# The partner rows of a rotary rotation: VectorE's shuffle, or two transfers from SBUF to SBUF

## The chip, the cores and the metric

The kernel runs on one core of a Trainium2 chip. A core has a matrix engine (TensorE, PE in the profile, with its weight loads as PEld), a vector engine (VectorE, DVE), an activation engine (ScalarE, ACT), GpSimd (POOL) and SyncE (SP), from whose queue (SPq) all transfers of this kernel are issued. Each engine runs its own list of instructions in order, and semaphores make one wait for another. Data lies in SBUF, 128 partitions wide; TensorE writes its results to banks of PSUM.

The metric is the device time of one execution in microseconds, the median of several runs. All arithmetic is in float32.

## The reference

Two transformer layers on an input of 2 x 1024 tokens with 512 features. In each layer the attention (16 heads of 32 features, causal) and a gated feed-forward block both read the same normalised input, and both results are added to x:

```python
x = L0_attn_X                                   # (2, 1024, 512)
xn = _layernorm(x, axis=-1)
x = x + attn0(xn) + ffn0(xn)                    # hidden width 2048
xn = _layernorm(x, axis=-1)
x = x + attn1(xn) + ffn1(xn)                    # hidden width 1408, scaled ternary weights
```

Queries and keys are rotated by position before the scores. The two layers pair the 32 features of a head in different ways:

```python
# layer 0: neighbours are a pair
x0 = x[..., 0::2]; x1 = x[..., 1::2]
r0 = cos * x0 - sin * x1
r1 = sin * x0 + cos * x1
return jnp.stack((r0, r1), axis=-1).reshape(x.shape)

# layer 1: feature d and feature d + 16 are a pair
x1, x2 = (x[..., :half], x[..., half:])
return jnp.concatenate([x1 * cos - x2 * sin, x1 * sin + x2 * cos], axis=-1)
```

Then follow `softmax(q k^T / sqrt(32))` under the causal mask, the product with the values, and the output projection.

## The kernel before

**Stages.** A phase is one layer for one of the two batch rows: four phases, layer 0 first. In each phase the 16 heads are worked in four groups of four, so that a group's 4 x 32 features fill the 128 partitions. Queries and keys are kept transposed, with features on the partitions and tokens along the columns: `qT` holds 512 tokens of a group in one tile, `kT` all 1024. A group's scores come in blocks of 256 queries, a block in steps of 256 keys: 10 steps for each group, 40 for each phase, 160 in all (class `Run`). A step makes the scores on TensorE (`sc`), copies them to SBUF (`s`), finds row maxima (`rmax`), subtracts them and takes exponentials. Five steps later (`LAG`) the weighted sums `av` are formed on TensorE. The row maxima of a block go out to DRAM (`md`) and come back spread over all partitions (`mb`), two transfers from SyncE's queue.

**Filling in.** Between the steps, the class `Fill` gives TensorE the rest of the phase's work: the projections to queries and keys (class `QueriesKeys`), to values, the hidden units of the feed-forward block (class `Hidden`), the down-projections `d` and the output projections. The projections and hidden units share the form `Unit`: four pieces, `first` to `fourth`, which get the four blocks of a product from seven half-size products of sums and differences. Intermediate results are copied from a PSUM bank by ScalarE into one of four buffers of 128x512 (`keep`, pool `t5_p`, names `p`, `u`, `raw`), while TensorE goes on to accumulate into the same bank.

**The rotation.** A `QueriesKeys` unit yields four tiles of 128x512 for a group: queries and keys, for the first and the second 512 tokens. Each goes through `rotated` (lines 864 to 880). `raw` is the tile of unrotated rows, one of the four `t5` buffers. For each group of 32 partitions, VectorE's `stream_shuffle` (line 877) writes into `swapped` (one of two buffers) the row's partner: the neighbour in layer 0, the row 16 further in layer 1, from the table `SWAP` (line 49). Then GpSimd multiplies `raw` by the cosines in place (line 878), VectorE multiplies `swapped` by the signed sines (line 879), and GpSimd adds both into `qT` or `kT` (line 880). There are four phases, four groups in each and four tiles in each group, thus 64 rotations. The first four (names `raw_k` and `raw_q`) come from `project_qk` at the start of the kernel; the 60 others come from the 15 units, with `raw` called `p_qk` (twice), `u_qk` and `raw_qk`. In the profile `swapped` is `sw_q` or `sw_k`. The tables of cosines and sines come from `rope_tables` (line 1761).

**The order of the work.** No order is written by hand for the engines. The class `Schedule` records each operation with the operations that it depends on, gives it a cost from a formula (`cost`, line 187), and lays out two plans by simulating the five engines: a first one while the program is being recorded, and a second one at its end (`again`, line 358), which orders each engine's queue by due times worked back from TensorE's ideal sequence. The instructions are then emitted in the order of the second plan's start times. Lines 208 and 209 hold the planned cost of a shuffle, 735 ns; line 193 that of a transfer: 450 ns of SyncE, and 1900 ns plus the bytes divided by 345 per ns until it lands, to which line 162 adds 900 ns until another engine sees it. The second plan may move GpSimd's additions to VectorE when they are late (`either`), and may bring forward one of the next seven pieces of TensorE's work when the next one would wait over 300 ns. A `View` (line 52) carries the region of a tile that an operation touches; `apart` (line 151) tells two regions that have nothing in common.

Of the kernel before, what the change touches and what calls it, by code (L numbers as in the profile page):

```python
# [19 lines left out]
B, T, D, H = 2, 1024, 512, 16  # L20
DH = D // H
# [22 lines left out]
def ts(n, size):  # L44
    return slice(n * size, (n + 1) * size)

SWAP = ([d ^ 1 for d in range(DH)], [(d + DH // 2) % DH for d in range(DH)])


class View:
# [5 lines left out]
    def __getitem__(self, idx):  # L58
        idx = idx if isinstance(idx, tuple) else (idx,)
        idx = idx + (slice(None),) * (len(self.shape) - len(idx))  # L60
        shape, region = [], []
        for n, i in zip(self.shape, idx):
            if isinstance(i, slice):
                a, b, _ = i.indices(n)
                shape.append(b - a)
                region.append((a, b))
            else:
                region.append((i, i + 1))
        return View(self.tile, self.chain + [("__getitem__", (idx,), {})], shape, self.region if self.chain else region)

    def rearrange(self, pattern, **sizes):
# [83 lines left out]
class Schedule:  # L155
# [31 lines left out]
    def cost(self, eng, method, args, kwargs, outs, ins):  # L187

        n = self.columns(outs[0]) if outs else 0
        if eng is self.sync:  # L190

            size = 4 * int(np.prod((outs or ins)[0].shape, dtype=int))
            return 450.0, 1900.0 + size / self.RATE
        if eng is self.tensor:
            if method == "transpose":
                mode, t = "full", 131.0
            else:
                lhs, rhs = args[1], args[2]
                small_k, small_m = lhs.shape[0] < P, lhs.shape[1] < P
                mode = "rows" if small_k else "columns" if small_m else "full"  # L200
                t = max(self.columns(rhs), 64) * 1.676 / (1 if mode == "full" else 4)
            if mode != self.mode:
                t += {"full": 218.0, "columns": 100.0, "rows": 200.0}[mode]
                self.mode = mode
            return t, t + 163.0
        m = max([n] + [self.columns(i) for i in ins])
        if eng is self.vector:
            if method == "stream_shuffle":
                t = 735.0
            elif method == "reciprocal":  # L210
                t = 204.0
            elif method == "tensor_reduce" and not kwargs.get("apply_transpose"):
                t = (150.0 if ins[0].tile.pool.psum else 110.0) + m * (0.93 if ins[0].tile.pool.psum else 1.85)
            elif method == "bn_aggr":
                t = 182.0
            else:
                t = 160.0 + m * 1.04
        elif eng is self.scalar:
            t = (190.0 if method == "activation" and args[2] in self.TABLES else 150.0) + 0.85 * n
            for k in ("bias", "scale"):  # L220
                t += 105.0 if isinstance(kwargs.get(k), View) else 0.0
            t += 140.0 if method == "mul" else 0.0
        elif method == "affine_select":
            t = 150.0 + 0.95 * n
        elif method in ("memset", "tensor_copy"):
            t = 100.0 + 1.16 * n
        else:
            t = 184.0 + 2.12 * n
        return t - self.BESIDE[eng.name], t
# [276 lines left out]
def two_layers(ctx: ExitStack, tc: tile.TileContext, x_in, attn_w, ffn_w, ffn_s, rope, out):  # L506
    ctx.enter_context(tc.manual_schedule())
    nc = Schedule(tc.nc)
# [64 lines left out]
    phases = [(layer, b) for layer in range(2) for b in range(B)]  # L573
# [288 lines left out]
    turned = {}  # L862

    def rotated(ph, g, which, half, raw):
        layer, _ = phases[ph]
        turned[ph, g] = turned.get((ph, g), 0) + 1
        name = f"{which}{ph}_{g}_{half}"
        if which == "q":
            dst = qT[ph, g, half] = q_p.tile([P, TB], F32, tag="q", name=f"{name}T")
        else:  # L870
            if (ph, g) not in kT:
                kT[ph, g] = k_p.tile([P, T], F32, tag="k", name=f"k{ph}_{g}T")
            dst = kT[ph, g][:, ts(half, TB)]
        cos, sin = tables[ph]
        cols = ts(half, TB)
        swapped = tmp.tile([P, TB], F32, tag="swapped", name=f"sw_{name}")
        nc.vector.stream_shuffle(swapped, raw, SWAP[layer])
        nc.gpsimd.tensor_tensor(raw, raw, cos[:, cols], ALU.mult)
        nc.vector.tensor_tensor(swapped, swapped, sin[:, cols], ALU.mult)
        nc.gpsimd.tensor_tensor(dst, raw, swapped, ALU.add)  # L880
# [3 lines left out]
    def project_qk(which, tokens):  # L884

        half, at = divmod(tokens.start, TB)
        n = tokens.stop - tokens.start
        ps = bank(f"ps_{which}0_{tokens.start}", (P, n))
        for c in range(DC):
            nc.tensor.matmul(  # L890
                ps, wqk[0, 0, which][:, c, :], xnT[0, half][:, c, at : at + n], start=(c == 0), stop=(c == DC - 1)
            )
        if tokens.stop == T:
            load_next_wqk(0, 0, which)
        if at == 0:
            raws[which] = t5_p.tile([P, TB], F32, tag="t5", name=f"raw_{which}0_{half}")
        nc.scalar.copy(raws[which][:, at : at + n], ps)
        if at + n == TB:
            rotated(0, 0, which, half, raws[which])

    class QueriesKeys(Unit):
# [11 lines left out]
        def c11(self, bank, one):  # L913
            nc.vector.tensor_tensor(one, bank, one, ALU.add)
            rotated(self.ph, self.g, "q", 0, one)

        def c22(self, bank, k1):
            nc.vector.tensor_tensor(k1, bank, k1, ALU.add)
            rotated(self.ph, self.g, "k", 1, k1)
# [496 lines left out]
    class Fill:  # L1416
# [14 lines left out]
        def add(self, cost, fn, kind="other", unit=None, slice_=0):  # L1431
            self.main.append((cost, fn, kind, unit, slice_))
# [40 lines left out]
        def do_main(self, step):  # L1473
            cost, fn, kind, unit, _ = self.main.pop(0)
            if kind == "first":
                self.unit = unit
            fn()
            if kind == "second":
                self.decide(step)
            if cost and kind != "alone":  # L1480
                self.turn = True
            return cost
# [196 lines left out]
    for i in range(total + LAG):  # L1679
        ph = min(i // per_phase, len(phases) - 1)  # L1680
# [5 lines left out]
        run, n = steps[i] if i < total else (None, 0)  # L1686
# [74 lines left out]
def rope_tables():  # L1761

    pos = np.arange(T, dtype=np.float32)
    half = np.arange(DH // 2, dtype=np.float32)
    base = np.float32(10000.0)
    freq0 = np.power(base, np.float32(-2.0) * half / np.float32(DH))
    freq1 = np.float32(1.0) / np.power(base, half / np.float32(DH // 2))
    d = np.arange(P) % DH
    tables = []
    for freq, pair, first in ((freq0, d // 2, d % 2 == 0), (freq1, d % (DH // 2), d < DH // 2)):  # L1770
        angles = (freq[pair][:, None] * pos[None, :]).astype(np.float32)
        sign = np.where(first, -1.0, 1.0).astype(np.float32)[:, None]
        tables.append(np.stack([np.cos(angles), np.sin(angles) * sign]))
    return np.ascontiguousarray(np.stack(tables), dtype=np.float32)

# [37 lines left out]
```

## Time and profile before

Three runs took 1810.8, 1814.7 and 1815.25 us; the median is 1814.7. The profiled execution:

| | us | share of the span |
|---|---|---|
| span of the profiled execution | 1812.9 | |
| TensorE busy (PE) | 1798.0 | 99% |
| VectorE busy (DVE) | 1476.3 | 81% |
| GpSimd busy (POOL) | 1232.6 | 68% |
| ScalarE busy (ACT) | 1041.7 | 57% |
| TensorE's granted clock, mean | 0.998 | |
| share of the 16 DMA engines' time, SyncE's queue | | 28.5% |

The profile page gives the span from the first to the last instruction; it has no figure for the time around it.

How to read it: the lines of groups name an engine, an operation, the tile written and the tiles read, the shape and the count, and then the busy time in us, the mean duration in ns, and the time for which the engine stood idle just before such instructions, with what ended it. All instructions recorded by `Schedule` carry the same line, L278, as its `call` issues them; so one goes by the tiles' names. A matmul of 512 columns in float32 appears as two instructions. The durations of matmuls contain the time in the pipeline, so two in a row overlap.

### The profile page before, as it was taken

Reading aid. Unit: us, or ns where it says so; the run is one execution under the profiler, and the core shown is the slowest. Engines: PE = TensorE matmul, PEld = TensorE weight load, DVE = VectorE, ACT = ScalarE, POOL = GpSimd, SP = SyncE. Lnnn points to the kernel's source line nnn. Section 1 sums busy time; section 2 is a strip of 40 time slices with the busy share of each in tenths; the row PEclk is TensorE's granted clock in tenths of the full one; section 3 lists DMA queues with packets and bytes.
Section 4 is the critical chain, followed back from the end, with each engine's and each line's share of the span. In section 5 each row is a group of like instructions: output and inputs, shape, how many; then the busy total and the mean of one; then the engine's idle time right before and its main releaser. Section 6 shows DMA issues by size and latency. Waiting matters only on the chain.

```text
span 1812.9 us, 25807 instructions
## 1 busy us (share of the span) xinstructions
PE 1798.0 (99%) x9406; PEld 880.0 (49%) x9406; DVE 1476.3 (81%) x1975; ACT 1041.7 (57%) x1240; POOL 1232.6 (68%) x1145
## 2 busy tenths in 40 slices
PE   9999999999999999999999999999999999999998
PEld 5464444444444644444444455444444464444443
DVE  3665988868879668779697798888979998989988
ACT  2444665556546565554575556576565757565762
POOL 6726875956868337446377894886779775866775
PEclk9999999999999999999999999999999999999999
DMA  5324343222232422222133324222223322221211
GB/s 192 99 82 137 114 148 120 67 80 82 80 113 88 138 72 68 70 82 89 56 97 102 115 76 160 76 80 71 77 84 98 125 69 71 70 69 50 67 39 71
DMA packets 140334, 165.15 MB, mean 91 GB/s; under 512 B 13360, under 2 KB 93488, under 8 KB 140208
## 3 DMA queue, kind: packets, MB, share of 16 engines
q1 hardware_dynamic: 140208, 163.50, 28.5%
q8 instruction: 75, 1.23, 0.3%
q14 instruction: 51, 0.42, 0.1%
HBM read 134.62 MB, written 28.84 MB: 90 GB/s over the span
## 4 chain that ended last, share of the span: by engine, by line
PE 89%; POOL 5%; DVE 3%; issue 1%; ACT 1%; DMA 1%; SPq 0%; POOLq 0%; ACTq 0%; DVEq 0%
PE d L278 24%; PE ux L278 19%; PE uy L278 9%; PE sc L278 8%; PE av L278 7%; PE ux_qk L278 5%; PE uz L278 5%; POOL acc L278 2%; PE uy_qk L278 2%; PE ux_v L278 2%; PE uz_qk L278 1%; PE uy_v L278 1%; DVE s L278 1%; PE ps_o L278 1%; PE tr L278 1%
## 5 line engine op out<-in xcount | busy, mean ns | idle before, releaser
L278 POOL TENSOR_TENSOR acc<-acc,s 128x512 f32<-128x512 f32 (+1 forms) x378 | 487.4, 1311 | 84.4 <-ACT s L278 79.9
L278 DVE TENSOR_TENSOR s<-s,mb 128x512 f32<-128x512 f32 (+1 forms) x384 | 489.6, 1300 | 12.5 <-DMA mb<-md 12.5
L278 DVE TRANSPOSE_TENSOR_REDUCE rmax<-s 128x32 f32<-128x1024 f32 (+1 forms) x320 | 351.5, 1117 | 63.9 <-POOL s L278 41.3
L278 PE MATMUL d<-wd,hT 128*128 128x512 f32 x864 | 400.1, 593 | 0.0
L278 ACT ACTIVATE s<-s 128x1024 f32<-128x1024 f32 (+1 forms) x320 | 304.9, 970 | 163.0 <-DVE s L278 161.0
L278 ACT ACTIVATE s<-sc 128x1024 f32<-128x1024 f32 (+1 forms) x320 | 283.3, 934 | 195.1 <-PE sc L278 184.0
L278 POOL TENSOR_TENSOR acc<-s 128x512 f32<-128x512 f32 (+1 forms) x128 | 169.2, 1328 | 195.3 <-ACT s L278 191.5
L278 PEld LDWEIGHTS d<-wd,hT 128*128 128x128 f32 x864 | 161.9, 190 | 192.6 <-issue 186.9
L278 ACT ACT_TABLE_LOAD x167 | 214.3, 1283 | 7.7 <-DVE s L278 4.7
L278 DVE TENSOR_TENSOR x<-d,x 128x512 f32<-128x512 f32 x224 | 151.3, 676 | 75.8 <-PE d L278 75.0
L278 PE MATMUL av<-s,v 128*32 128x256 f32 (+1 forms) x2560 | 159.2, 364 | 0.7 <-ACT s L278 0.5
L278 POOL TENSOR_SCALAR_AFFINE_SELECT s<-s 128x512 f32<-128x512 f32 x128 | 98.9, 784 | 67.0 <-ACT s L278 65.0
L278 PEld LDWEIGHTS av<-s,v 128*32 128x32 f32 x2560 | 67.6, 109 | 145.7 <-issue 97.2
L278 POOL TENSOR_TENSOR hT<-p,hT 128x512 f32<-128x512 f32 x53 | 72.5, 1367 | 77.9 <-ACT hT L278 77.9
L278 PE MATMUL d<-wo,oT 128*128 128x512 f32 x198 | 103.0, 602 | 1.2 <-DVE hT L278 1.2
L278 PE MATMUL ux<-xs,ws 128*128 128x512 f32 x212 | 101.7, 602 | 0.6 <-ACT p L278 0.6
L278 PE MATMUL ux<-xnT,wu 128*128 128x512 f32 x212 | 101.8, 602 | 0.1
L278 PE MATMUL ux<-xnT,wg 128*128 128x512 f32 x212 | 100.9, 598 | 0.4 <-DVE hT L278 0.4
L278 PE MATMUL ux<-xs,wu 128*128 128x512 f32 x212 | 101.2, 600 | 0.0
L278 PE MATMUL uy<-xs,ws 128*128 128x512 f32 x212 | 99.7, 593 | 0.3 <-DVE hT L278 0.3
L278 PE MATMUL uy<-xnT,ws 128*128 128x512 f32 x212 | 99.8, 593 | 0.0
L278 PE MATMUL uz<-xnT,wg 128*128 128x512 f32 x212 | 99.7, 593 | 0.0
(179 smaller groups left out, 2511.2 us busy)
## 6 DMA issues: line engine op xcount, KB each, us to landing
mb<-md SPq DMA_DIRECT2D x64, 512.0 KB, 3.8
wg<-in_gate SPq DMA_DIRECT2D x54, 256.0 KB, 2.9
wd<-in_down SPq DMA_DIRECT2D x32, 256.0 KB, 2.9
xr<-xm SPq DMA_DIRECT2D x32, 256.0 KB, 2.7
wu<-in_up SPq DMA_DIRECT2D x28, 256.0 KB, 3.0
s12gu<-ws SPq DMA_DIRECT2D x26, 256.0 KB, 2.0
ws<-s12gu SPq DMA_DIRECT2D x26, 256.0 KB, 2.6
wd<-wds SPq DMA_DIRECT2D x22, 256.0 KB, 2.9
```

Source lines behind the costliest of these rows:

```text
L278: target(*[get(a) for a in args], **{k: get(a) for k, a in kwargs.items()})
```

## The change

The shuffle is replaced by two transfers on SyncE's queue. The first writes the even rows of `swapped` from the odd rows of `raw`, the second the odd rows from the even ones: 64 rows of 2 KB each. For this the partner of every row has to be its neighbour in both layers. So the columns of the second layer's query and key weights are laid out on the host so that features d and d + 16 of a head become neighbours, and the tables of cosines and sines use the layer 0 arrangement for both; scores are sums over the features of a head, which the order of the features doesn't alter. `View` learns steps, so that the plan sees the two transfers as touching different rows, and the planned cost of the shuffle is dropped. The transfers get the planned cost of any other transfer.

```diff
-SWAP = ([d ^ 1 for d in range(DH)], [(d + DH // 2) % DH for d in range(DH)])
...
     def __getitem__(self, idx):
...
             if isinstance(i, slice):
-                a, b, _ = i.indices(n)
-                shape.append(b - a)
+                a, b, step = i.indices(n)
+                shape.append(len(range(a, b, step)))
                 region.append((a, b))
+                if step > 1:
+                    parity = (a % step, a % step + 1)
...
+        if parity:
+            region.append(parity)
...
         if eng is self.vector:
-            if method == "stream_shuffle":
-                t = 735.0
-            elif method == "reciprocal":
+            if method == "reciprocal":
                 t = 204.0
...
         swapped = tmp.tile([P, TB], F32, tag="swapped", name=f"sw_{name}")
-        nc.vector.stream_shuffle(swapped, raw, SWAP[layer])
+        for a in range(2):
+            nc.sync.dma_start(out=swapped[a::2, :], in_=raw[1 - a :: 2, :])
         nc.gpsimd.tensor_tensor(raw, raw, cos[:, cols], ALU.mult)
         nc.vector.tensor_tensor(swapped, swapped, sin[:, cols], ALU.mult)
         nc.gpsimd.tensor_tensor(dst, raw, swapped, ALU.add)
...
-    for freq, pair, first in ((freq0, d // 2, d % 2 == 0), (freq1, d % (DH // 2), d < DH // 2)):
-        angles = (freq[pair][:, None] * pos[None, :]).astype(np.float32)
-        sign = np.where(first, -1.0, 1.0).astype(np.float32)[:, None]
+    for freq in (freq0, freq1):
+        angles = (freq[d // 2][:, None] * pos[None, :]).astype(np.float32)
+        sign = np.where(d % 2 == 0, -1.0, 1.0).astype(np.float32)[:, None]
...
+    for w in "qk":
+        halves = arrays[f"w{w}1"].reshape(D, H, 2, DH // 2)
+        arrays[f"w{w}1"] = halves.transpose(0, 1, 3, 2).reshape(D, D)
```

More of the change, by code (lines that the diff above doesn't have):

```diff
@@ L60, in __getitem__ @@
         idx = idx + (slice(None),) * (len(self.shape) - len(idx))
-        shape, region = [], []
+        shape, region, parity = [], [], None
         for n, i in zip(self.shape, idx):
             if isinstance(i, slice):
-                a, b, _ = i.indices(n)
-                shape.append(b - a)
+                a, b, step = i.indices(n)
+                shape.append(len(range(a, b, step)))
                 region.append((a, b))
+                if step > 1:
+                    parity = (a % step, a % step + 1)
             else:
                 region.append((i, i + 1))
+        if parity:
+            region.append(parity)
         return View(self.tile, self.chain + [("__getitem__", (idx,), {})], shape, self.region if self.chain else region)
@@ L864, in rotated @@
     def rotated(ph, g, which, half, raw):
-        layer, _ = phases[ph]
         turned[ph, g] = turned.get((ph, g), 0) + 1
```

## The prediction

> **What bounds the kernel now.** I read the page's totals first, then who TensorE waits for, then the busy times by stretch, then the groups that the change touches.
>
> ```profile
> span 1812.9 us, 25807 instructions
> ...
> PE 1798.0 (99%) x9406; PEld 880.0 (49%) x9406; DVE 1476.3 (81%) x1975; ACT 1041.7 (57%) x1240; POOL 1232.6 (68%) x1145
> ```
>
> TensorE is busy for 1798.0 of 1812.9 us. All its idle time is 14.9 us, so no relief of another engine can bring more than that. What it waits for, in the list of its own waits (us in total, times, longest):
>
> ```profile
> PE av L278 <- DVE sums L278: 3.1, 7, 1.1
> PE tr L278 <- ACT xn L278: 2.0, 1, 2.0
> ...
> PE d L278 <- DVE hT L278: 1.2, 1, 1.2
> ...
> PE ux L278 <- ACT p L278: 0.6, 1, 0.6
> PE av L278 <- ACT s L278: 0.5, 2, 0.3
> PE ux L278 <- DVE hT L278: 0.4, 1, 0.4
> PE uy L278 <- DVE hT L278: 0.3, 1, 0.3
> ```
>
> The four waits on VectorE come to 3.1 + 1.2 + 0.4 + 0.3 = 5.0 us; none is on a DMA. By stretch (us of the stretch; then busy us and instructions of PE, PEld, DVE, ACT, POOL; clock, DMA share, GB/s):
>
> ```profile
> 45.00:500.00 455.00, 455.00 (x2190) 221.06 (x2191) 347.34 (x456) 253.91 (x305) 313.45 (x307) 1.00 0.32 101
> 1340.00:1400.00 60.00, 59.42 (x368) 28.92 (x361) 57.06 (x77) 34.38 (x45) 53.56 (x50) 1.00 0.31 95
> 1400.00:1500.00 100.00, 95.84 (x609) 54.23 (x608) 95.62 (x127) 66.91 (x80) 77.11 (x65) 1.00 0.30 94
> 1760.00:1813.00 53.00, 46.93 (x246) 19.82 (x244) 45.67 (x65) 18.74 (x22) 34.01 (x29) 0.98 0.17 60
> ```
>
> Through the first phase TensorE never stops and VectorE has a quarter of its time free. Only where the last phase opens, 1340 to 1500, is VectorE full (57.06 + 95.62 = 152.7 of 160 us), and there TensorE loses 0.6 + 4.2 us. The rest of its idle time is the start (4.2 us to 45) and the end (6.1 us after 1760), which the rotation hardly touches: the last rotation ends at 1687.
>
> **Part 1, the shuffles go.** By shape (busy us, mean ns, idle before):
>
> ```profile
> L278 DVE STREAM_SHUFFLE sw_k<-p_qk 128x512 f32<-128x512 f32 x15 | 11.1, 740 | 0.0
> L278 DVE STREAM_SHUFFLE sw_q<-u_qk 128x512 f32<-128x512 f32 x15 | 11.0, 735 | 0.1
> L278 DVE STREAM_SHUFFLE sw_k<-raw_qk 128x512 f32<-128x512 f32 x15 | 11.0, 735 | 0.0
> L278 DVE STREAM_SHUFFLE sw_q<-p_qk 128x512 f32<-128x512 f32 x15 | 11.0, 732 | 0.0
> ```
>
> With two each of raw_q and raw_k (1.5 + 1.5 us) that is 64 shuffles and 47.1 us of VectorE, which falls to about 1429 us. On the path it is worth at most the 5.0 us that TensorE waits for VectorE. Of these 2.7 + 0.4 + 0.3 = 3.4 us lie between 1335 and 1510, where two units' eight shuffles (5.9 us) go. I take half of that: **-1.7 us**; bounds 0 and -5.0.
>
> **Part 2, each rotation takes longer.** No row moves data from SBUF to SBUF. The nearest are 128 KB transfers between SBUF and DRAM (KB each, median us from issue to landing):
>
> ```profile
> s3gu<-wu SPq DMA_DIRECT2D x26, 128.0 KB, 1.7
> ...
> wk<-s3qk SPq DMA_DIRECT2D x7, 128.0 KB, 2.0
> wk<-in_wk SPq DMA_DIRECT2D x7, 128.0 KB, 2.3
> ```
>
> The last two are a pair like the new one: at 1391.59 and 1391.95 SyncE issues them back to back, 0.36 apart, and the second lands 2.3 us after its issue, 2.7 us after the first. Bounds for the new pair: 1.7 us (a short store, the issues free) and 0.36 + 2 x 2.3 = 5.0 us (one after the other). I take 2.7, as this row is a pair of the same size on the same queue. Against 0.735 for the shuffle, rotation grows by **1.9 us** (bounds 1.0 and 4.2). Also, cos times raw writes raw in place, so GpSimd now waits until both transfers have read it, where it waited for the shuffle.
>
> The Trainium skill, "DMA: Bandwidth & Descriptors", section "Rules for kernel authors", speaks against such a pair: two transfers to disjoint halves of the partitions serialize, since both spread over the same 16 DMA engines, and one transfer of 128 partitions should be used. By that rule I would put the pair near the upper bound, 5.0 us; the pair of loads in this trace, whose second landing came 0.7 us behind a lone one's 2.0, does not show it so strongly.
>
> What covers 1.9 us? First, the scores that need the rotated rows. Inside a phase there is ample cover: k_2T is complete at 246.1 and first read at 292.3; k_3T at 355.5 and 411.5. Where phases open, k_0T is complete at 521.5 and read at 526.6; 1011.8 and 1017.6; so 5.1 and 5.8 us. At the third opening it is complete at 1420.4 and read at 1420.6, but there the shuffle had ended at 1403.2 and its product with sin sat in VectorE's queue until 1418.4, so 15 us of cover stand ahead of it. In the last group, complete at 1687.0 and read at 1691.3: 4.3 us. All exceed 1.9.
>
> Second, raw is one of four t5 buffers. While it is held, the next unit's copy of a PSUM bank can't start, and the product that accumulates in that bank waits on TensorE. One place shows this already, at the third opening:
>
> ```profile
> 1398.92 0.58 ACT L278 COPY p<-ux 128x512 f32<-128x512 f32 x1 [6.74 <-POOL q_0T L278]
> ...
> 1399.56 1.98 PE L278 MATMUL ux<-xs,ws 128*128 128x512 f32 x4 [0.58 <-ACT p L278]
> ```
>
> ScalarE stood 6.74 us for q_0T's sum, and TensorE 0.58. Here 1.9 us more has no cover: **+1.9**. The other units show no such wait, as the planner puts down-projections in between; if they lost their cover too, 15 units x 1.9 = 28.5 is the upper bound. The lower is 0 (the planner moves a down-projection here too).
>
> **Part 3, SyncE's queue.** 128 issues at 0.32 to 0.46 us are 41 to 59 us of its time and 16.8 MB on 163.5, so about 2.9 points on the DMA share of 28.5%. They come into the queue that carries the row maxima out and back (md, mb). VectorE waits for mb ten times, 12.5 us. If a rotation's two issues (0.7 us) stood ahead of all ten: +7 us for VectorE, the upper bound; 0 if they fall elsewhere. TensorE doesn't wait for mb at all, and one in ten is my choice: **+0.7**.
>
> **Part 4, GpSimd.** The two products, with cos and with sin, now start at one landing. The products with cos show a median of 1.27 us in one group (p_qk) and 1.73 in another (u_qk), the price when VectorE works beside them: up to 64 x 0.46 = 29 us on an engine with 580 us free, and TensorE's waits for GpSimd are one of 1.4 us at the start. **0**; without the cover it would be part of the 28.5 above.
>
> **Part 5, the plan.** The order of every queue is computed from costs, so all of it is laid out anew. TensorE's 16 score products of one step take 0.94 us in some steps and 1.15 in others, for what stands beside them; 14 of 160 steps changing kind are 3 us. **0**, bounds -3 and +3. The second layer's weight columns are laid out before the launch and change no instruction.
>
> **Sum**: -1.7 + 1.9 + 0.7 = +0.9, so 1813.8 for an execution like the profiled one (the page gives its span, 1812.9, and no time around it). That span lies 1.8 below the median of the runs, 1814.7, whose spread is 1810.8 to 1815.25; on the median it makes **1815.6, forecast 1816**.
>
> **Rivals.** What a measurement of this kernel can tell from no change is 0.3%, 5.4 us: faster is below 1809.3, slower above 1820.1.
>
> (a) *Raw's buffers become the wait* (slower). Each unit's four rotations hold their t5 buffer 1.9 to 4.2 us longer, ScalarE's copy stands as at 1398.92, and TensorE stands behind it. For: the four buffers are just the four that one query-key unit uses, so the next unit stands on them; one stall is there already. Against: TensorE has no such wait in the 14 other units. It decides from half the units on: 7.5 x 1.9 = 14 us, 1829; with all 15, 1843. If the pair doesn't overlap (the change then isn't a swap by two transfers side by side), 7.5 x 4.2 = 32 us, 1846.
>
> (b) *SyncE's queue* (slower). It runs in order; a transfer that waits there for raw, or for one of the two swapped buffers that GpSimd's sum frees, holds all behind it, mb and weights among them. For: SyncE already waits long for single events (53 waits on m, 177.4 us). Against: only 12.5 us of that reach VectorE. With 2.7 us of hold-up per rotation unit reaching TensorE in four of the 15 units and at the start: 5 x 2.7 = 13.5 us, 1828.
>
> (c) *VectorE was the limit of the tight stretch* (faster). All 5.0 us of TensorE's waits for it go, and the new plan saves the 3 us of part 5: 1814.7 - 8.0 = 1807. For: 95.62 of 100 us busy from 1400 to 1500. Against: the same stretch has the stall of part 2.
>
> **Chances.** Forecast (within 0.3%) 0.42; (a) 0.22; (b) 0.16; (c) 0.20. So faster 0.20, same 0.42, slower 0.38. The forecast's own range is 1810 to 1820. As both signs hold much, the range goes to (c)'s 1807 short of its end, and to (a) and (b) at 1829: 1808 to 1830, which leaves out about a tenth on each side.
>
> **What would show it.** Right: no shuffle rows, VectorE's busy near 1429, 128 transfers of 128 KB landing within 1.7 to 2.7 us, TensorE busy near 1798 with waits below 17 us. (a) would show as ACT p or u waiting for q_0T, q_1T or k sums in many units and TensorE behind them; (b) as longer waits of s on mb; (c) as TensorE's waits on sums and hT gone from 1400 to 1500. The forecast is wrong if TensorE's busy time itself moves by more than 3 us, by another order of its products.

## The result and the profile after

Nine runs of the changed kernel took 1815.6 to 1818.96 us, median 1816.5. Nine runs of the kernel before took 1810.61 to 1815.25, median 1811.09. The ratio is 1.0025, 95% interval 1.0016 to 1.0034: some 4.5 us slower by the ratio (the two medians lie 5.4 apart), inside the 0.3% that the prediction calls no change, if barely by the medians, and outside what the runs leave to chance. Three executions in the experiments below, of 2094.84 us in e7, 6524.11 in e8 and 5398.35 in e9 (the one that was profiled), are of a rare slow kind and left out of the ratios.

The totals of the page of the changed kernel:

```profile
span 1813.1 us, 26038 instructions
...
PE 1794.3 (99%) x9406; PEld 878.5 (48%) x9406; DVE 1432.1 (79%) x1846; ACT 1039.9 (57%) x1237; POOL 1221.9 (67%) x1147
```

VectorE has lost 44 us of work, and TensorE's share is as before. The span looks like that of the execution shown before (1812.9), but the two can't be set side by side. That one began with TensorE at 0.92 of its clock in the first 45 us, and made its first scores at 44.00 us; the changed kernel's has 1.00 there and makes them at 40.71. A second profile of the same five queues with the clock at 1.00 (experiment e4 below) makes them at 41.03 and spans 1809.8 us. That is the one to compare with: 3.3 us more in the span, of which TensorE's busy time gives -0.6 (1794.9 to 1794.3) and its idle time +3.9 (14.9 to 18.8). The profile of the changed kernel is that of the shortest of its nine executions: its span is 1813.1 us at a mean clock of 1.000, while the other eight have 1813.5 to 1816.2 (the median of all nine is 1814.0) at 0.997 to 0.999. An execution also lasts 2.5 us longer than its span (median), where that of the order of before lasts 1.9 longer (e4). So 0.9 + 0.6 us of the difference lie outside what this profile shows, and were not traced.

Where that idle time lies, by stretch; first the order of before, from e4 (us of the stretch, then busy us of PE, PEld, DVE, ACT, POOL, clock, DMA share, GB/s):

```profile
1340.00:1400.00 60.00, 59.44 (x339) 28.49 (x338) 57.08 (x77) 35.59 (x46) 55.80 (x52) 1.00 0.29 91
1400.00:1500.00 100.00, 95.87 (x609) 54.22 (x608) 96.46 (x125) 66.95 (x80) 74.82 (x63) 1.00 0.29 92
...
1760.00:1813.00 53.00, 44.02 (x226) 18.61 (x224) 42.59 (x63) 15.69 (x17) 30.94 (x28) 0.99 0.17 60
```

and the changed kernel:

```profile
45.00:500.00 455.00, 454.30 (x2187) 220.15 (x2186) 338.30 (x433) 247.33 (x299) 312.40 (x309) 1.00 0.35 108
...
1340.00:1400.00 60.00, 59.76 (x344) 28.97 (x343) 55.85 (x71) 37.10 (x48) 50.67 (x49) 1.00 0.39 119
1400.00:1500.00 100.00, 94.48 (x572) 52.46 (x571) 88.97 (x109) 67.17 (x79) 80.12 (x69) 1.00 0.35 108
...
1760.00:1813.00 53.00, 45.63 (x242) 19.70 (x241) 44.67 (x65) 17.83 (x20) 33.64 (x29) 0.99 0.17 60
```

From 1400 to 1500 VectorE went from 96.46 busy us to 88.97, and TensorE stands idle longer, not less: 5.5 us for 4.1. The end costs 7.5 us for 5.8 (1813.1 - 1760 - 45.63, and 1809.8 - 1760 - 44.02). The first phase, without a gap before, now has 0.7. So VectorE was relieved just where it was full, and the path gained nothing. The largest piece of the 3.9 us is the end's 1.7, where no rotation runs (the last is over at 1691); e3 below, which has neither shuffles nor transfers, loses 7.3 us there. What TensorE waits for now (us in total, times, longest):

```profile
PE av L279 <- ACT s L279: 4.1, 3, 2.2
PE av L279 <- DVE sums L279: 3.1, 6, 0.9
PE sc L279 <- POOL k_0T L279: 1.9, 1, 1.9
...
PE d L279 <- DVE x L279: 0.7, 2, 0.5
PE ux_v L279 <- DVE v L279: 0.6, 1, 0.6
```

Before, `av` waited 0.5 us for ScalarE's `s`, and `sc` not for `k_0T`. Of these lines only the third is a wait for a rotated tile, and its transfers are not what made it late: at the third opening of a phase they are issued at 1395.91, but the product with the sines comes at 1418.94, 23 us later in VectorE's queue:

```profile
1395.91 1.11 SPq L279 DMA_DIRECT2D sw_k<-raw_qk  x2
...
1418.94 0.68 DVE L279 TENSOR_TENSOR sw_k<-sw_k,sin 128x512 f32<-128x512 f32 x1
...
1419.70 1.26 POOL L279 TENSOR_TENSOR k_0T<-raw_qk,sw_k 128x512 f32<-128x512 f32 x1 [0.74 <-DVE sw_k L279]
...
1421.01 0.94 PE L279 MATMUL sc<-q_0T,k_0T 32*128 32x256 f32 x16 [1.87 <-POOL k_0T L279]
```

The transfers themselves (KB each, median us from issue to landing):

```profile
sw_q<-p_qk SPq DMA_DIRECT2D x30, 128.0 KB, 2.1
sw_k<-p_qk SPq DMA_DIRECT2D x30, 128.0 KB, 2.0
sw_q<-u_qk SPq DMA_DIRECT2D x30, 128.0 KB, 2.2
sw_k<-raw_qk SPq DMA_DIRECT2D x30, 128.0 KB, 2.4
```

They land 2.0 to 2.4 us after their issue, and an issue takes 0.53 us (median), so a pair is complete 2.5 to 2.9 us after it began (taken pair by pair, the median of all 64 is 2.6; those at the kernel's start are the slowest, up to 6.8). VectorE waits for these transfers 18.9 us in all (6.7, 3.7, 3.5, 2.9 and 2.1, by groups), which is part of why 44 us less work helps so little, and TensorE for none. VectorE waits for mb in sum as before, 12.6 us for 12.5.

### The profile page after: what moved, and what is told of

Its sections match the earlier page's. It is cut to its first block, busy times and chain, and to the rows that moved or that the text cites. A ratio compares the mean times of both kernels' runs of the same rounds, so it can differ in the third digit from the quotient of the medians.

```text
span 1813.1 us, 26038 instructions
## 1 busy us (share of the span) xinstructions
PE 1794.3 (99%) x9406; PEld 878.5 (48%) x9406; DVE 1432.1 (79%) x1846; ACT 1039.9 (57%) x1237; POOL 1221.9 (67%) x1147
## 4 chain that ended last, share of the span: by engine, by line
PE 90%; DVE 4%; POOL 3%; issue 1%; ACT 1%; DMA 1%; SPq 0%; POOLq 0%; DVEq 0%
PE d L279 23%; PE ux L279 19%; PE uy L279 9%; PE sc L279 8%; PE av L279 7%; PE ux_qk L279 5%; PE uz L279 5%; PE ux_v L279 3%; PE uy_qk L279 2%; POOL acc L279 2%; DVE s L279 1%; PE uy_v L279 1%; PE uz_qk L279 1%; PE ps_o L279 1%; DVE rmax L279 1%
## 5 line engine op out<-in xcount | busy, mean ns | idle before, releaser
L279 DVE TENSOR_TENSOR s<-s,mb 128x512 f32<-128x512 f32 (+1 forms) x384 | 492.5, 1308 | 12.7 <-DMA mb<-md 12.6
```

The lines of the kernel that those rows point to most:

```text
L279: target(*[get(a) for a in args], **{k: get(a) for k, a in kwargs.items()})
```

## The experiments

The theories. **L**, the longer way: readers of `swapped` and `raw` come late. **P**, the plan: with another cost in it, the planner lays the whole program out anew, and the new order is a few us worse, whatever the swap is done with. In the change both come together. The emission of an operation can be changed behind the planner's back, and the planner's price can be changed with no instruction changed; so they can be taken apart.

**e1, the old plan with transfers.** The weights' layout is that of the change; the plan is made with the shuffle, and its place is taken by two transfers when the instructions are written. All engines but SyncE, and VectorE without its shuffles, keep the order of before.

```diff
         def call():
+            if method == "stream_shuffle":
+                o, i = args[0].real(), args[1].real()
+                for a in range(2):
+                    self.nc.sync.dma_start(out=o[a::2, :], in_=i[1 - a :: 2, :])
+                return
```

> The plan of the kernel before, made with a shuffle of 735 ns, but each planned shuffle is issued as the two transfers; every engine keeps its order, TensorE's products included. Theory P (the changed kernel is slower because the order of the work was laid out anew, not because of the transfers): ratio to before 0.999 to 1.001. Theory L (the way over the DMA engines is longer, and readers of swapped and of raw come late): ratio 1.002 or more, as the plan left no room for a longer way, with VectorE's and GpSimd's waits on transfers of sw_q and sw_k of 60 to 120 us in sum, 64 x 1 to 2.

Measured: 1857.6 us, ratio 1.0254 (1.0240 to 1.0268). P's expectation missed; L holds in this plan, with ten times the size of the change. Who waits for the transfers:

```profile
DVE sw_q L286 <- DMA sw_q<-u_qk: 28.6, 10, 4.5
...
DVE sw_k L286 <- DMA sw_k<-raw_k: 18.8, 2, 10.0
POOL p_qk L286 <- DMA sw_q<-p_qk: 18.6, 5, 7.7
...
DVE sw_q L286 <- DMA sw_q<-p_qk: 16.9, 8, 3.8
...
POOL p_qk L286 <- DMA sw_k<-p_qk: 14.8, 9, 2.8
DVE sw_k L286 <- DMA sw_k<-raw_qk: 13.7, 7, 3.9
```

With two smaller VectorE groups (2.7, 1.0) and three GpSimd ones (10.0, 9.1, 5.6) that is 82 us of VectorE and 58 us of GpSimd, more than the 60 to 120 expected, at the heads of their queues with all else behind. TensorE's idle time is spread over the whole kernel:

```profile
45.00:500.00 455.00, 443.98 (x2139) 214.07 (x2138) 324.69 (x418) 246.16 (x297) 306.49 (x299) 1.00 0.33 105
```

11.0 us are lost in the first phase, where the order of before loses none. Over the whole span TensorE is idle 29 us longer than in e4 and busy 17 us longer, at a mean clock of 0.995. So the cost of the longer way is real; the changed kernel, whose plan knows of it, has little of it: 18.9 us of VectorE's waits and 16 of GpSimd's for 82 and 58.

**e2, the new plan with shuffles.** The reverse: the plan of the changed kernel, and one shuffle at the place of the first of each two transfers.

```diff
+        pair = method == "dma_start" and isinstance(kwargs["out"], View) and kwargs["out"].tile.tag == "swapped"
         def call():
+            if pair:
+                if not hasattr(kwargs["out"].tile, "turned"):
+                    kwargs["out"].tile.turned = True
+                    o, i = kwargs["out"].tile.get(), kwargs["in_"].tile.get()
+                    self.nc.vector.stream_shuffle(o, i, [d ^ 1 for d in range(DH)])
+                return
```

> The plan of the changed kernel, made with transfers, but each pair is issued as one shuffle on VectorE at the place of the first transfer; TensorE, ScalarE and GpSimd keep the changed kernel's order. Theory P: ratio to before 1.002 to 1.004, as the changed kernel. Theory L: the long way is gone, so ratio 1.000 or below; VectorE's 47 us come back where the plan did not expect them, which costs at most 5 us, ratio 1.003.

Measured: 1820.7 us, ratio 1.0047 (1.0034 to 1.0059). In the same order of work the shuffles are slower than the transfers, not faster, and the changed kernel's marks are here without any transfer:

```profile
PE av L287 <- ACT s L287: 4.1, 3, 2.2
...
PE sc L287 <- POOL k_0T L287: 1.3, 1, 1.3
```

The wait for `s` is the same to a tenth of a us, that for `k_0T` nearly. So the order brings these waits with it, and the transfers' longer way is not needed for them. L's expectation, at most 1.003, missed; P's, 1.002 to 1.004, was right in direction and a little low. The cut is not clean: e2 takes the longer way out and puts VectorE's 47 us in at once, and the changed kernel's order with neither was not run. What makes e2 0.22% or 4 us slower than the changed kernel is not shown. VectorE's 47 us, put where the plan had no room for them, are one candidate; the granted clock is another: in e2's profile it is 0.97 in the mean from 1400 to 1500, and TensorE is busy 2.6 us longer in all (1796.9 for 1794.3) and idle 3.4 longer (22.2 for 18.8).

**e3, no swap at all.** The product with the sines reads `raw`. Planned anew.

```diff
-        for a in range(2):
-            nc.sync.dma_start(out=swapped[a::2, :], in_=raw[1 - a :: 2, :])
...
-        nc.vector.tensor_tensor(swapped, swapped, sin[:, cols], ALU.mult)
+        nc.vector.tensor_tensor(swapped, raw, sin[:, cols], ALU.mult)
```

> The swap is left out: the product with the sines reads raw itself, so rotation lacks its partner rows. Neither shuffle nor transfer; the plan is made anew without them. If VectorE's 47 us are worth something on the path, this is the most that any swap off VectorE can bring: ratio to before 0.997 to 0.999 (my -1.7 to -5 us). Theory P: anything within 0.998 to 1.003, as the plan decides. Theory L: below the changed kernel by at least 3 us.

Measured: 1815.25 us, ratio 1.0021 (1.0012 to 1.0030). With neither shuffles nor transfers the kernel is as slow as the changed one, and slower than with shuffles in the old plan. My expectation of 0.997 to 0.999 missed: whatever VectorE's 47 us brought, this new plan took away. L's expectation, 3 us below the changed kernel, missed too: it is 1.2 us by the medians, 0.7 by the ratios. This is a plan of its own, so it can't price the longer way alone.

**e4, the layout alone.** The change's layout of the columns, with the shuffle on neighbours in both layers; all five queues have the order of before.

```diff
-        for a in range(2):
-            nc.sync.dma_start(out=swapped[a::2, :], in_=raw[1 - a :: 2, :])
+        nc.vector.stream_shuffle(swapped, raw, [d ^ 1 for d in range(DH)])
```

(beside it, the shuffle's price of 735 ns stays in the plan)

> The second layer's columns in pairs, with the shuffle kept and one table of neighbours for both layers; all five queues in the order of the kernel before. Both theories: ratio 0.9995 to 1.0005. Its trace also shows the plan of before a second time, so that a start with another clock can be told from the rest.

Measured: 1812.1 us, ratio 1.0003 (0.9994 to 1.0012). The layout is free.

**e5, e6, e11, the price of the shuffle.** In the kernel before, one number of the plan is changed; the instructions are the same, and stand in another order.

```diff
             if method == "stream_shuffle":
-                t = 735.0
+                t = 710.0        # e6: 760.0, e11: 725.0
```

> The kernel before with one number changed: the plan takes a shuffle for 710 ns, not 735 (the trace has 728 to 740). No instruction is added or removed; 182 of TensorE's 2129 rows, 305 of VectorE's, stand in another place. Theory P, in its strong form (any new plan is slower than the one before by about 0.2%, as that was a lucky one): ratio 1.0015 to 1.004. Theory V (the new plans are slower because the swap left VectorE; a plan with a shuffle is as good as before): 0.999 to 1.001.

> As the one before, with 760 ns; 177 of TensorE's rows stand in another place, and not the same ones. Strong P: ratio 1.0015 to 1.004; V: 0.999 to 1.001. If the two differ from each other by more than 0.1%, the size of the change's effect is that of the draw among plans.

> The kernel before with the shuffle planned at 725 ns: a third plan of the same instructions; 183 rows of TensorE stand elsewhere. After 710 (ratio 1.0007) and 760 (1.0024): theory P expects 1.000 to 1.003, seldom below 1.

Measured: 710 ns, 1812.75 us, ratio 1.0007 (0.9998 to 1.0016); 760 ns, 1815.9 us, 1.0024 (1.0015 to 1.0033); 725 ns, 1831.6 us, 1.0111 (1.0098 to 1.0125). V, that a plan with a shuffle is as good as before, falls with the last two; that any new plan costs 1.0015 to 1.004, the strong form of P, misses for the first and the third. The spread among plans of one and the same program is four times the effect of the change, and wider than I expected.

Where e11 loses most of its 20 us is the stretch that was tight before:

```profile
1060.00:1340.00 280.00, 280.00 (x1574) 140.42 (x1573) 237.60 (x324) 171.67 (x202) 202.26 (x194) 1.00 0.28 88
1340.00:1400.00 60.00, 57.55 (x309) 26.71 (x306) 55.22 (x72) 34.67 (x44) 50.04 (x48) 1.00 0.34 100
1400.00:1500.00 100.00, 89.27 (x485) 47.30 (x486) 86.66 (x109) 61.05 (x71) 73.46 (x59) 0.88 0.26 80
```

TensorE is idle for 2.5 + 10.7 = 13.2 us of these 160, 8.5 more than in e4; and the granted clock falls to 0.88 over 100 us, which by my estimate is another 0.12 x 89.27 = 10.7 us of slower work. Both make 19.2 of the 20.9 us between the two spans (1830.7 and 1809.8). The estimate is high: by the totals TensorE is busy only 8.1 us longer (1803.0 for 1794.9), and of 12.8 us more idle time 4.3 lie in other stretches. The gaps are the same kind as the changed kernel's, in TensorE's rows of the timeline:

```profile
1400.99 1.92 PE L278 MATMUL av<-s,v 128*32 128x256 f32 x12 [2.63 <-ACT s L278]
...
1418.36 0.28 PE L278 MATMUL av<-sums,fold 128*32 128x8 f32 x4 [1.98 <-DVE sums L278]
1421.09 1.93 PE L278 MATMUL av<-s,v 128*32 128x256 f32 x16 [2.45 <-ACT s L278]
```

Why this order comes late there and that of 710 ns doesn't, was not traced further.

**e7, e8, e12, the price of the transfers.** In the changed kernel, the plan's cost for the rotation's transfers alone.

```diff
             size = 4 * int(np.prod((outs or ins)[0].shape, dtype=int))
+            if outs and outs[0].tile.tag == "swapped":
+                return 530.0, 1300.0          # e8: 450.0, 2100.0 + size / self.RATE
+                                              # e12: 450.0, 1890.0 + size / self.RATE
             return 450.0, 1900.0 + size / self.RATE
```

> The changed kernel, with the transfers of the rotation planned at what the trace of it shows: 530 ns of SyncE, and 2.2 us until an engine sees them, where the plan had 450 ns and 3.2 to 3.6 us. 80 of TensorE's rows stand elsewhere. Theory P: within 0.9985 to 1.002 of the changed kernel, either way, as it is one more draw. If too long a planned latency is what costs (theory L'), it is faster than the changed kernel by 2 us or more: ratio to before below 1.0015. If the plan's surplus of latency is what keeps the transfers harmless, slower: above 1.004.

> The changed kernel, with the rotation's transfers planned 200 ns longer (2100 ns plus bytes, not 1900). 90 of TensorE's rows stand elsewhere. Theory P: ratio to before 1.000 to 1.004, another draw; L' (planned latency costs): above the changed kernel's 1.0025 by 0.1% or more.

> The changed kernel with its transfers planned 10 ns shorter; 15 of TensorE's rows and 63 of VectorE's stand elsewhere. Theory P: ratio to before 1.001 to 1.004, near the changed kernel, as most of its plan stays. Nothing else in it differs.

Measured: e7 1819.3 us, ratio 1.0040 (1.0026 to 1.0053); e8 1816.3 us, 1.0022 (1.0013 to 1.0032); e12 1821.2 us, 1.0052 (1.0039 to 1.0064). L', that a planned latency above the measured one costs, falls: the plan nearest to what the trace shows is not faster than the changed kernel's, and the one further from it is not slower. e7 stands on the border of its third expectation, that the plan's surplus of latency keeps the transfers harmless (above 1.004); e12, too, has less surplus and is slower, so this is not ruled out. e12 differs from the changed kernel by 10 ns of price, which moves 15 of TensorE's operations in the plan, and is 0.27% slower; I had expected at most 1.004.

**e9, the queue's load alone.** The order of before with its shuffles, and beside each, two transfers into a spare tile that nothing reads. SBUF had room for 1.5 KB a row. `self.still` is the table of cosines in DRAM.

```diff
         def call():
+            if method == "stream_shuffle":
+                t = self.spare.tile([P, 384], F32, tag="spare", name=f"spare{op.seq}")
+                for a in range(2):
+                    self.nc.sync.dma_start(out=t[a::2, :], in_=self.still[1 - a :: 2, 0:384])
```

> The plan of the kernel before, shuffles kept, and beside each shuffle two transfers more on SyncE's queue (64 rows of 1.5 KB each, from the table of cosines in DRAM into a spare tile that nothing reads). This is the load on the queue and the DMA engines alone, in a plan that doesn't know of it. My step of SyncE's queue: 64 x 2 issues put 0 to 7 us on VectorE's waits for mb, at most 0.7 us on the time: ratio to before 0.999 to 1.001. If the queue made the 46 us of the old plan with transfers: above 1.01.

Measured: 1811.4 us, ratio 0.9999 (0.9990 to 1.0008). 128 transfers more on SyncE's queue cost nothing that can be measured, even in a plan that doesn't know of them.

**e10, raw held.** The same, but the transfers read `raw` (`in_=i[1 - a :: 2, 0:384]`, with `i` the shuffle's source).

> As the one before, but the transfers read raw: SyncE's queue waits until raw is there, and GpSimd's product with the cosines, which writes raw in place, waits until they have read it. VectorE's product with the sines still reads what the shuffle wrote. If the wait of GpSimd and the hold on SyncE's queue are half of the 46 us: ratio to before 1.01 or more. If nearly all of it is VectorE standing before its product with the sines: 1.000 to 1.005.

Measured: 1847.5 us, ratio 1.0190 (1.0176 to 1.0204). That is 34 of the 46 us of e1, and the expectation that VectorE's wait before the sines would be nearly all of it missed. VectorE doesn't wait for these transfers; GpSimd does, as its product with the cosines overwrites `raw`:

```profile
POOL p_qk L286 <- DMA spare<-p_qk: 24.6, 14, 3.8
...
POOL raw_k L286 <- DMA spare<-raw_k: 8.9, 2, 6.5
...
POOL u_qk L286 <- DMA spare<-u_qk: 5.7, 6, 1.4
```

With raw_qk (4.0) and raw_q (1.3) these are 44.5 us of GpSimd at the head of its queue. GpSimd's lateness is handed on to ScalarE, which can't copy into a `t5` buffer before the rotation that holds it has its sum:

```profile
ACT p L286 <- POOL q_0T L286: 6.8, 1, 6.8
ACT u L286 <- POOL q_1T L286: 5.5, 1, 5.5
ACT raw_qk L286 <- POOL q_1T L286: 5.2, 1, 5.2
ACT raw_qk L286 <- POOL k_3T L286: 5.1, 1, 5.1
```

That is 22.6 us, where the kernel before has the first line's 6.7 alone; behind it TensorE waits 3.9 us for copies to p and u, after 0.6. SyncE's queue is also held here until `raw` is there, and waits 20.8 us for earlier transfers into the one spare buffer, which e1 doesn't have. VectorE's wait for mb, 14.6 us against 12.5, and the absence of any wait of TensorE for a transfer speak for GpSimd's wait as the larger share, but the two were not taken apart.

No version was faster than the kernel before. Nine kernels have another plan than it (e2, e3, e5 to e8, e11, e12, and the changed kernel, whose plan e2 shares); their ratios run from 1.0007 to 1.0111. The plan of before is a good draw from this set; a plan better than it was not found.

## Why the prediction was right, and where it was not

The forecast, no change within 0.3%, came out, at 1816.5 us for 1816. That the time is so near is luck: the sum said +0.9 on a median of 1814.7, and it was +4.5 (by the ratio) on 1811.09, so a base 3.6 too high and a change 3.6 too small cancel. The base was too high, since two of the three runs shown, and the profiled one, were among the longer of those that nine runs now show; in the profiled one the slow start of TensorE accounts for 3 us (44.00 against 41.03 for the first scores).

**What bounds the kernel.** Right: TensorE stays at 99%, and the relief of VectorE could bring no more than its idle time.

**Part 1, the shuffles go (-1.7).** VectorE's busy time fell to 1432.1, forecast 1429. TensorE's waits for VectorE are 3.1 + 0.7 + 0.6 + 0.3 + 0.2 + 0.2 = 5.1 us, after 5.0: none of it went. e3 says the same with nothing in the shuffles' place: 5.3 us for sums alone. The term is 0.

**Part 2, the longer rotation (+1.9).** The price of the pair was right: 2.7 us forecast from the pair of loads, 2.5 to 2.9 measured, so the two transfers largely overlap. (2.7 less 0.735 is 2.0, not 1.9; it changes nothing.) By the rule of the Trainium skill that was weighed against it ("DMA: Bandwidth & Descriptors", "Rules for kernel authors"), two transfers to disjoint halves of the partitions serialize; one after the other they would have taken near 5.0, the prediction's estimate, and at 128 KB the trace doesn't show that. The place was wrong: ScalarE's 6.7 us for q_0T, on which 1.9 us were to be added, are no longer in the list of waits. The cover that was named for the other rotations held: the one wait for k_0T at the third opening is there with a shuffle too (e2). On the path the term is 0, as far as e2 and e3 can tell.

**Part 3, SyncE's queue (+0.7).** 0 by e9; and the wait for mb went from 12.5 to 12.6 us. An issue costs 0.53 us (median of each group), more than the 0.32 to 0.46 taken from other transfers.

**Part 4, GpSimd (0).** 0 in the new plan, where GpSimd waits 16 us for the transfers (6.1, 3.4, 3.2 and 3.1, by groups). What the cover is worth if it is gone was named as part of 28.5 us; e10, where SyncE's queue is held as well, puts it at 34. Thus rivals (a) and (b) were right to take a plan that doesn't fit as the danger, and left out where it begins: at GpSimd, standing before a product that overwrites what a transfer still reads (44.5 us in e10). The t5 buffers of (a) come behind it, with 22.6 us of ScalarE; the share of (b), SyncE's queue held by a transfer that waits, was not separated.

**Part 5, the plan (0, bounds -3 and +3).** This is the step that failed, by its size. It was taken from the two durations of a step's score products, in other words from TensorE's busy time, which moved by only 0.6 us. What an order costs is in TensorE's waits, and in some orders in a lower granted clock beside them; there e5, e6 and e11 show +1.3 to +20 us for one inert number, where the bounds were 3 either way. With 0, 0, 0 and 0 for the others, this term is the +4.5, as the remainder.

**Rival (c)** fell: VectorE got 7.5 us of relief between 1400 and 1500 and TensorE's idle time there rose.

What stays open: why the new orders wait for `s` and `sums` where the last phase opens; what the transfers' longer way costs by itself in the changed kernel's own order; and whether any plan with the transfers is as good as that of before.

## What to carry to other kernels

Where a planner lays out the whole program from prices, a change has two effects: its own, and another draw of the order. Before a few tenths of a per cent are credited to the change, move an inert price by some per cent and see how far the time moves; and keep the order while the instructions change, to see the change alone. A transfer in place of an instruction on an engine costs little if the order leaves its latency room, and 2.5% here where it didn't; look first at the instruction that overwrites what the transfer reads.

## What the runs showed of the hardware that was not expected

An issue of one of these transfers, 64 rows at every other partition, takes 0.53 us (median) of SyncE's queue; the issues of whole tiles and of contiguous halves in the trace of before take 0.32 to 0.48 by the medians of their groups. Some other transfers of 128 KB land later in the changed kernel (wk from s3qk 2.8 us after its issue, 2.0 before; s3gu from wu 2.2, 1.7 before), others do not (wu from s3gu 2.1 in both).

A gap of 2.63 us on TensorE was followed by a lower granted clock. In e11, by stretches of 10 us:

```profile
1390.00:1400.00 10.00, 8.36 (x23) 3.29 (x21) 9.88 (x12) 5.42 (x7) 8.93 (x9) 1.00 0.43 132
1400.00:1410.00 10.00, 9.01 (x38) 4.16 (x39) 5.53 (x8) 5.40 (x7) 5.67 (x5) 0.66 0.07 27
...
1440.00:1450.00 10.00, 8.37 (x36) 4.13 (x35) 6.24 (x10) 4.05 (x5) 3.54 (x5) 0.59 0.01 1
1450.00:1460.00 10.00, 10.00 (x52) 4.53 (x50) 9.69 (x11) 7.60 (x9) 8.11 (x5) 1.00 0.43 131
```

The clock (third figure from the end) is 0.66 in the stretch that begins with that gap, and 16 score products at 1402.84 take 2.09 us, where 0.94 to 1.15 is usual; it is 1.00 again in the stretch from 1450, which has no gap. The length of a gap alone doesn't decide it. In the profile of the changed kernel a gap of 2.21 us and one of 1.87, 4 us apart, left the clock at 1.00. In e2, in the same order of work, the same 2.21 and one of 1.27 were followed by a clock of 0.72 and then 0.59:

```profile
1420.58 0.63 PE L287 MATMUL av<-s,v 128*32 128x256 f32 x4 [2.21 <-ACT s L287]
...
1424.08 1.66 PE L287 MATMUL sc<-q_0T,k_0T 32*128 32x256 f32 x16 [1.27 <-POOL k_0T L287]
...
1420.00:1425.00 5.00, 2.83 (x24) 1.38 (x28) 4.54 (x7) 1.47 (x2) 4.26 (x4) 0.72 0.28 105
1425.00:1430.00 5.00, 5.00 (x19) 2.29 (x16) 3.03 (x3) 0.63 (x2) 3.59 (x3) 0.59 0.39 106
```

And in e7 a gap of 1.88 us, with no other from 1030 to 1100, was followed by 0.66:

```profile
1064.94 2.47 PE L281 MATMUL ux<-xs,wu 128*128 128x512 f32 x4 [1.88 <-DVE p L281]
...
1065.00:1070.00 5.00, 5.00 (x32) 1.95 (x36) 5.00 (x6) 4.27 (x5) 5.00 (x6) 0.66 0.52 157
1070.00:1075.00 5.00, 5.00 (x31) 3.78 (x24) 4.65 (x5) 3.31 (x5) 5.00 (x4) 1.00 0.00 0
```

What decides it, these runs don't settle. One profile with the clock at 1.00 therefore doesn't show that a gap is harmless: the changed kernel's eight other executions have a mean clock of 0.997 to 0.999. An order that stalls TensorE by some 2 us may pay twice.
